# A mixture-of-experts layer and a Fourier layer: each row block's sum stays in on-chip memory from its gathers to its placing

## The chip, the cores and the metric

The kernel runs on one core of one Trainium2 chip. The metric is the device time in microseconds (us), the median of three runs. The engines are named as in the profile: PE multiplies matrices, PEld is its loading of weights, DVE, ACT and POOL work on vectors, and SP issues DMAs. On-chip memory has 128 partitions; DRAM is the memory outside. All arithmetic is float32.

## The reference

Two layers follow each other. The input `x` is 32 x 128 x 56 x 56.

```
layer 0:  x  = depthwise_conv7x7(input) + bias;  x = layernorm over channels -> xf [100352, 128]
          logits = xf @ Wg; the two best of 8 experts per token, softmax weights
          each expert takes at most cap = 15680 tokens, in order of priority -> slot of (token, choice)
          y  = gelu(buf @ W1[e] + b1[e]) @ W2[e] + b2[e]        per expert e, buf = rows of xf
          out0 = input + x + layer_scale * sum over 2 choices of  gate * y[slot]
layer 1:  feat = gelu(batchnorm(conv3x3, dilation 3 (out0)))     128 -> 64 channels
          F2   = fft2(feat); channel attention per head on F2; gate = sigmoid(two 1x1 convs of real(F2))
          out  = concat(|ifft2(attn @ F2)|, |ifft2(gate * F2)|) + out0
```

What this case is about is the line `out0`: for each token the normed row of `xf` and two rows of `y`, which lie at arbitrary slots, are added and transposed back to channels by pixels.

## The kernel before

**Layer 0.** The convolution, the norm and the routing leave `xf` (one row of 128 floats per token) and, after them, two lists `slot1` and `slot2`. The experts run one after the other in chunks of 512 slots: `first_layer` (L1071) and `second_layer` (L1089) on PE, GELU on ACT; `y`, already times its gate and the layer's scale, goes to the DRAM tensor `yf`. Row 0 of `yf` is zero, for tokens that found no room.

**Row blocks.** An image has 7 blocks of 8 rows; two images make a pair, 16 pairs in all, and block `r` (0 to 111) is the same 8 rows of both images of its pair: 7 tiles of 128 tokens. For each block `release` (L442) issues 14 gathers on POOL, one per call (L458: 128 rows of `yf` by `slot1` or `slot2`), into two tiles `y` of [128, 7, 128]. Ahead of a block's first gather it takes a tile `xa` from the pool `d6` and loads the block's rows of `xf` into it (L451, SP). `total` (L465) adds both `y` to `xa` on DVE (L474, two instructions of 896 elements in each partition) and stores the sum to the DRAM tensor `xsum` (L475, SP). Later `bring(r)` (L490) reads the block back from `xsum` into a tile `xs` of the pool `d3`, which has three buffers (L497, SP).

**Placing.** `place(r)` (L1282) transposes the 7 tiles of `xs` on PE (L1289) and adds them on DVE to the padded images `xp` (L1293), which then are the input of layer 1.

**Layer 1.** `front` places the 7 blocks of a pair and runs the 3x3 convolution on them (L1304). `back` is the Fourier part: `transform` alternates transposes on PE (L1347), copies from PSUM on DVE (`mid`, L1334), products on PE (L1355) and copies on ACT (L1358), four times; between them the attention (L1444, L1445) and the gate (L1482). The steps of the next pair's `front` are fed in between those of this pair's `back`. Outputs leave by SP (L1461, L1530).

**What sets the order.** PE, DVE, ACT and POOL each execute their own list in order, and so does SP for its DMAs. A planner places the instructions of a list by their dependencies; the kernel adds rules. `worked` (L482) counts columns of PE work and calls `release` once for each PACE of them (684 columns, L1543), then `totals`, which sums a block when the gathers asked for have passed its end by 7. Each gather waits on POOL for the PE instruction that was the newest when the gather 16 places earlier was asked for (`marks`, `gated`). In the last expert's chunks `ahead` (L505) releases gathers too, as far as the finished slots allow. If a block is to be brought and its gathers have not all been asked for, `total` asks for the missing ones at once (L468). The sums stand on DVE behind the newest DVE instruction named in `step["dve"]`.

Of the kernel before, what the change touches and what calls it, by code (L numbers as in the profile page):

```python
# [30 lines left out]
F32 = mybir.dt.float32  # L31
# [7 lines left out]
C = 128  # L39
# [6 lines left out]
E = 8  # L46
# [5 lines left out]
NB = H // P8  # L52
# [22 lines left out]
def conv_seq_kernel(ctx: ExitStack, tc: tile.TileContext, t: dict, out: bass.AP, dbg: dict):  # L75
    nc = tc.nc
    NI = t["xp"].shape[0]
    HI = NI // 2
    J = HI * NP
# [24 lines left out]

    xf = dram.tile([J * 128, C], F32, name="xf")
    yf = dram.tile([NSLOT + 1, C], F32, name="yf")
    xs_ = dram.tile([J * 128, C], F32, name="xsum")
    xl = dram.tile([-(-cap // 512) * 512, C], F32, name="xlast")
    xfv = xf.rearrange("(j p) c -> p j c", p=128)
    xsv = xs_.rearrange("(j p) c -> p j c", p=128)  # L110
    xlv = xl.rearrange("(j p) c -> p j c", p=128)


# [12 lines left out]
    with tc.tile_pool(name="a1", bufs=1) as a1, tc.tile_pool(name="a2", bufs=2) as a2, tc.tile_pool(  # L126
        name="a4", bufs=4
# [292 lines left out]
    begun_ = {}  # L420
    marks = []
    leash = {"n": 4}
    made_ = {"asked": 0, "summed": 0, "rows": 0}
    rows = {}
    step = {}
    work = {"since": 0}
# [15 lines left out]
    def release():  # L442

        n = made_["asked"]
        if n >= NRB * NG:
            return
        made_["asked"] += 1
        r, k = divmod(n, NG)
        if k == 0:
            xs = d6.tile([128, NB, C], F32, name="xa", tag="xa")  # L450
            nc.sync.dma_start(out=xs, in_=xfv[:, r * NB : (r + 1) * NB, :])  # L451
            begun_[r] = xs, []
        if k % NB == 0:
            begun_[r][1].append(d6.tile([128, NB, C], F32, name="y"))
        m = k % NB
        s = (slot1, slot2)[k // NB]
        marks.append(step["pe"])
        gated(marks[max(0, n - leash["n"])], nc.gpsimd.indirect_dma_start(  # L458
            out=begun_[r][1][-1][:, m, :],
            out_offset=None,  # L460
            in_=yf[: 1 + reach(r), :],
            in_offset=bass.IndirectOffsetOnAxis(ap=s[:, r * NB + m : r * NB + m + 1], axis=0),
        ))

    def total():  # L465

        r = made_["summed"]
        while made_["asked"] < (r + 1) * NG:  # L468
            release()
        made_["summed"] += 1  # L470
        xs, ys = begun_.pop(r)
        with tc.issue_after(step["dve"].ins):
            for y in ys:
                nc.vector.tensor_tensor(out=xs, in0=xs, in1=y, op=ALU.add)  # L474
        nc.sync.dma_start(out=xsv[:, r * NB : (r + 1) * NB, :], in_=xs)  # L475

    def totals(lag):

# [9 lines left out]
            totals(NB)  # L488

    def bring(r):  # L490
        if r >= NRB or r < made_["rows"]:
            return
        made_["rows"] = r + 1
        while made_["summed"] <= r:
            total()
        xs = rows[r] = d3.tile([128, NB, C], F32, name="xs")
        nc.sync.dma_start(out=xs, in_=xsv[:, r * NB : (r + 1) * NB, :])  # L497

    def inputs(pr):
        xps = [d4.tile([C, XL], F32, name="xp") for i in range(2)]  # L500
# [24 lines left out]
    if True:  # L525
# [649 lines left out]
        for e in range(E):  # L1175
            todo = late
            chain["on"] = e >= early
            if e + 1 < E:
                todo = todo + [due(1.4, lambda e=e: scale(e + 1))]
            if e in pairs:  # L1180
                todo = todo + search(*pairs[e])
            if e == E - 1:
                for s in late:
                    s()
                locate()
                lists_.close()
                rkey.__exit__(None, None, None)
                d4 = ctx.enter_context(tc.tile_pool(name="d4", bufs=4))
                d6 = ctx.enter_context(tc.tile_pool(name="d6", bufs=6))
                d3 = ctx.enter_context(tc.tile_pool(name="d3", bufs=3))  # L1190
                d0 = ctx.enter_context(tc.tile_pool(name="d0", bufs=1))
                first_inputs = inputs(0)
                bC = load(d0, "beta", [C, 1], t["ln_beta"].rearrange("(c o) -> c o", o=1))
                eps5 = d0.tile([128, 1], F32, name="eps5")
                norms = [[load(d0, n, [128, 5], t[n])] for n in ("bn1", "cgbn")]
                for i, n in enumerate(norms):
                    n += [d0.tile([128, 1], F32, name=f"{k}{i}") for k in ("scale", "shift")]
                cw = load(d0, "cw", [C, 9, DD], t["conv_w"])
                g1 = load(d0, "g1", [128, 32], t["cg1"])
                g2 = load(d0, "g2", [128, 128], t["cg2"])  # L1200
                g2b = load(d0, "g2b", [128, 1], t["cg2_b"])
                tau = load(d0, "tau", [128, 1], t["tau"])
                neg = load(d0, "neg", [128, 128], t["neg"])
                meanw = load(d0, "meanw", [128, 128], t["meanw"])
                rw = load(d0, "rw", [2 * W, 4 * KF], t["rw"])
                rh = load(d0, "rh", [2 * H, 4 * KF], t["rh"])
                ih = load(d0, "ih", [4 * KF, 2 * H], t["ih"])
                iw = load(d0, "iw", [4 * KF, 2 * W], t["iw"])
                todo = []
            if e + 1 < E - 1:  # L1210
                ids2, gates2 = lists()
                steps, late = listing(e + 1, ids2, gates2)
                todo = todo + steps
            elif e + 1 < E:
                (ids2, gates2), late = last, []
            if e == 0:
                todo = todo + search(E - 1, 1)
            if e == early - 1:
                last = [c1.tile([128, NC], d, name=n) for d, n in ((I32, "ids_last"), (F32, "gates_last"))]
                steps, done_ = listing(E - 1, *last)  # L1220
                todo = todo + steps + done_
            slots_ = len(chunks) * 4 - 18
            state = [0, 0, 0.0, 0]
            whole = sum(share.get(f, 0.7) for f in todo)

            def tick():
                state[0] += 1
                if e == E - 1:
                    state[2] += 1
                    ahead(i, state[2])  # L1230
                with tc.issue_after(step["dve"].ins):
                    while state[1] < len(todo) and state[2] * slots_ < state[0] * whole:
                        s = todo[state[1]]
                        if s in apart and state[3] == state[0]:
                            break
                        s()
                        state[2] += share.get(s, 0.7)
                        state[1] += 1
                        state[3] = state[0]

            for i, c0 in enumerate(chunks):
                if i + 1 < len(chunks):
                    then = fetch(ids, chunks[i + 1], e == E - 1)
                elif e + 1 < E:
                    then = fetch(ids2, 0, e + 1 == E - 1)
                if early <= e < E - 1 and i + (e - early) * len(chunks) < NC:
                    put(0, i + (e - early) * len(chunks))
                state[2] = 0 if e == E - 1 else state[2]
                if e == E - 1 and i == len(chunks) // 2:
                    batchnorms()  # L1250
                if e == E - 1 and i == len(chunks) - 1:
                    for r in range(2):
                        bring(r)
                ns, xT = now
                hT, gelu, mine = first_layer(e, ns, xT, tick)
                if left:
                    after, more = second_layer(*left, tick)
                    after(gelu)
                    mine = mine + more
                spots.append(mine + mine[-1:] * (8 - len(mine)))  # L1260
                left = e, c0, gates, ns, hT
                now = then
            assert state[1] == len(todo)
            if e + 1 < E:
                ids, gates = ids2, gates2
# [15 lines left out]

    def place(r, xps):  # L1282
        xs, rb = rows.pop(r), r % NB
        for m0 in range(0, NB, 4):
            nm = min(4, NB - m0)
            pt = bank("pxs")
            pv = pt[:, : nm * 128].rearrange("p (q m s) -> p q m s", m=nm, s=P8)
            for m in range(nm):
                nc.tensor.transpose(pv[:, :, m, :], xs[:, m0 + m, :], ident)  # L1289
            for i in range(2):  # L1290
                px = interior(xps[i], rb * P8, P8)[:, :, m0 * P8 : (m0 + nm) * P8]
                pi = pv[:, i * P8 : (i + 1) * P8].rearrange("p r m s -> p r (m s)")
                step["dve"] = nc.vector.scalar_tensor_tensor(  # L1293
                    out=px, in0=pi, scalar=bC, in1=px, op0=ALU.add, op1=ALU.add
                )
# [400 lines left out]
```

## Time and profile before

| | |
|---|---|
| median of three runs | 5173.07 us (5170.29 to 5176.02) |
| the profiled execution, its time / its span | 5216.56 us / 5214.8 us |
| mean granted PE clock | 0.943 of full speed |
| busy share of the span: PE, DVE, ACT, POOL | 89%, 54%, 40%, 50% |
| gathers of `y` on POOL (L458) | 1568, mean 990 ns |
| sums on DVE (L474) | 224 instructions, mean 1086 ns |
| `xa` loads, `xsum` stores, `xs` loads | 112 of each, 448 KB each |

One execution was profiled; its time is 43.5 us above the median of the runs that were timed without a profile. The last expert's gathers begin at 2605 us, the first placing stands at 2888 us, and the last gather starts at 5075.6 us. `back` runs L1403 once for each pair; from its first instance (2980.9 us) to its fifteenth (5042 us) lie 14 whole pairs. In rows of a stretch, the number behind an engine's busy time is its count of instructions in that stretch, "PEclk" is the mean granted clock, and "DMA" is the mean busy share of the 16 DMA engines.

### The profile page before, as it was taken

Reading aid. Unit: us, or ns where it says so; the run is one execution under the profiler, and the core shown is the slowest. Engines: PE = TensorE matmul, PEld = TensorE weight load, DVE = VectorE, ACT = ScalarE, POOL = GpSimd, SP = SyncE. Lnnn points to the kernel's source line nnn. Section 1 sums busy time; section 2 is a strip of 40 time slices with the busy share of each in tenths; the row PEclk is TensorE's granted clock in tenths of the full one; section 3 lists DMA queues with packets and bytes.
Section 4 is the critical chain, followed back from the end, with each engine's and each line's share of the span. In section 5 each row is a group of like instructions: output and inputs, shape, how many; then the busy total and the mean of one; then the engine's idle time right before and its main releaser. Section 6 shows DMA issues by size and latency. Waiting matters only on the chain.

```text
span 5214.8 us, 87254 instructions
## 1 busy us (share of the span) xinstructions
PE 4650.3 (89%) x33034; PEld 3232.1 (62%) x33034; DVE 2816.8 (54%) x5863; ACT 2079.1 (40%) x4260; POOL 2616.5 (50%) x2633
## 2 busy tenths in 40 slices
PE   8888845999999999999988899899988888888889
PEld 7777734777776777777766455555555555445556
DVE  4787887868675746442222345455544444444446
ACT  3676751444444444444433133333332222232224
POOL 0000023545555656666366566666666666665650
PEclk9999966999999999999999899999999999998999
DMA  9988840222222323333455456555555555555552
GB/s 255 271 260 262 262 127 26 65 64 66 68 69 71 86 76 85 88 86 93 149 156 133 115 158 163 155 149 149 147 154 152 155 155 158 150 130 146 157 142 57
DMA packets 767737, 705.23 MB, mean 135 GB/s; under 512 B 73232, under 2 KB 679569, under 8 KB 763221
## 3 DMA queue, kind: packets, MB, share of 16 engines
q1 hardware_dynamic: 597060, 487.55, 31.6%
q0 software_dynamic: 81664, 167.15, 14.6%
q10 hardware_dynamic: 88592, 44.96, 3.0%
q8 instruction: 261, 4.28, 0.4%
q14 instruction: 160, 1.30, 0.1%
HBM read 472.99 MB, written 226.39 MB: 134 GB/s over the span
## 4 chain that ended last, share of the span: by engine, by line
PE 70%; another core or an unknown queue 5%; issue 5%; DVE 4%; ACT 2%; DMA 0%; POOL 0%; DVEq 0%; ACTq 0%; POOLq 0%
PE py L1089 16%; PE ph L1071 15%; PE pf L1304 15%; PE pm L1355 9%; PE pt L1347 4%; PE pxt L1054 2%; PE pg L1379 2%; PE pre L1444 2%; PE pxs L1289 2%; PE pim L1445 2%; DVE junk L716 1%; PE pid L956 1%; PE pn L745 1%; DVE mid L1334 1%
## 5 line engine op out<-in xcount | busy, mean ns | idle before, releaser
L458 POOL DMA_INDIRECT y<-yf,slot x1568 | 1552.4, 990 | 971.3 <-issue 357.3
L1048 POOL DMA_INDIRECT xg<-xf,ids x861 | 906.9, 1053 | 689.2 <-PE py L1089 214.7
L1089 PEld LDWEIGHTS py<-W,hT 128*128 128x128 f32 x7872 | 928.9, 193 | 128.6 <-issue 108.2
L1089 PE MATMUL py<-W,hT 128*128 128x128 f32 x7872 | 948.7, 277 | 23.6 <-issue 23.3
L1304 PE MATMUL pf<-xp,cw 128*64 128x448 f32 x4032 | 926.7, 569 | 8.8 <-DVE xp L1293 6.1
L1071 PE MATMUL ph<-xT,W 128*128 128x512 f32 (+1 forms) x1984 | 907.3, 597 | 1.8 <-issue 1.8
L1074 ACT ACTIVATE hT<-ph,b1t 128x512 f32<-128x512 f32 (+1 forms) x992 | 616.2, 672 | 97.7 <-PE ph L1071 52.4
L1334 DVE COPY mid<-pt 112x512 f32<-112x512 f32 (+3 forms) x480 | 311.1, 662 | 570.5 <-PE pt L1347 239.4
L1123 ACT ACTIVATE yo<-yo,gates 128x128 f32<-128x128 f32 x861 | 275.3, 390 | 851.7 <-DVE yo L1103 782.3
L1103 DVE TENSOR_TENSOR yo<-py,b2t 128x512 f32<-128x512 f32 (+2 forms) x256 | 170.6, 669 | 790.1 <-issue 475.0
L1071 PEld LDWEIGHTS ph<-xT,W 128*128 128x128 f32 x1984 | 359.6, 193 | 339.2 <-issue 325.4
L1304 PEld LDWEIGHTS pf<-xp,cw 128*64 128x64 f32 x4032 | 289.8, 140 | 439.0 <-issue 394.7
L220 POOL TENSOR_SCALAR y<-y,sd,nb 128x128 f32<-128x128 f32 x49 | 24.8, 525 | 690.5 <-PE plq L277 689.2
L1358 ACT COPY T<-pm 128x464 f32<-128x464 f32 (+2 forms) x240 | 123.6, 520 | 494.3 <-PE pm L1355 282.6
L225 ACT ACTIVATE y<-y,nb,sd 128x128 f32<-128x128 f32 x735 | 287.6, 481 | 33.4 <-DVE nb L212 33.4
L1293 DVE SCALAR_TENSOR_TENSOR xp<-pxs,beta,xp 128x256 f32<-128x256 f32 x448 | 173.6, 445 | 169.7 <-remote 49.4
L174 PE MATMUL psa<-xt,stay 112*64 112x98 f32 (+1 forms) x4608 | 234.3, 262 | 34.6 <-DVE y L182 16.6
L174 PEld LDWEIGHTS psa<-xt,stay 112*64 112x64 f32 (+1 forms) x4608 | 220.0, 146 | 44.6 <-DVE y L182 23.1
L1312 ACT ACTIVATE feat<-pf,shift,scale 128x448 f32<-128x448 f32 x112 | 81.2, 725 | 411.7 <-remote 141.5
L474 DVE TENSOR_TENSOR xa<-xa,y 128x896 f32<-128x896 f32 x224 | 243.3, 1086 | 2.8
L1355 PE MATMUL pm<-ih,mid 116*128 116x112 f32 x928 | 151.0, 311 | 91.5 <-ACT T L1358 36.6
L1355 PEld LDWEIGHTS pm<-ih,mid 116*128 116x128 f32 x928 | 129.3, 215 | 165.9 <-issue 62.1
(410 smaller groups left out, 6241.9 us busy)
## 6 DMA issues: line engine op xcount, KB each, us to landing
xt<-in_x_dram SPq DMA_DIRECT2D x256, 392.0 KB
yf<-yo SPq DMA_DIRECT2D x240, 256.0 KB
xp<-in_xp_dram SPq DMA_DIRECT2D x32, 1832.0 KB
xa<-xf SPq DMA_DIRECT2D x112, 448.0 KB
xsum<-xa SPq DMA_DIRECT2D x112, 448.0 KB
xs<-xsum SPq DMA_DIRECT2D x112, 448.0 KB
xf<-y ACTq DMA_DIRECT2D x42, 1024.0 KB
y<-yf,slot POOLq DMA_INDIRECT x1568
```

The source lines that it names most:

```text
L174: nc.tensor.matmul(ps[h * 64 : (h + 1) * 64, c * TG : (c + 1) * TG], lhsT=wts[b][:, c4 + c, :], rhs=xv[: PKS[b], c, h, :, b * NB : b * NB ...
L225: nc.scalar.activation(yi, yi, AF.Identity, scale=sd[:, i : i + 1], bias=nb[:, i : i + 1])
L458: gated(marks[max(0, n - leash["n"])], nc.gpsimd.indirect_dma_start(out=begun_[r][1][-1][:, m, :], out_offset=None, in_=yf[: 1 + reach(r), :],
L474: nc.vector.tensor_tensor(out=xs, in0=xs, in1=y, op=ALU.add)
L1048: paced(2 * q, nc.gpsimd.indirect_dma_start(out=xg[:n, q, :], out_offset=None, in_=xf, in_offset=bass.IndirectOffsetOnAxis(ap=ids[:n, c0 + ...
L1071: step["pe"] = nc.tensor.matmul(ph[:, :ns], lhsT=W1[:, e, f * C : (f + 1) * C], rhs=xT[:, :ns], start=True, stop=True)
L1074: gelu = nc.scalar.activation(hT[:, f, :ns], ph[:, :ns], AF.Gelu, bias=b1t[:, e, f : f + 1])
L1089: step["pe"] = nc.tensor.matmul(py[:n, q * C : (q + 1) * C], lhsT=hT[:, f, q * 128 : q * 128 + n], rhs=W2[:, e, f, :], start=(f == 0), sto ...
L1123: nc.scalar.activation(yo[:n, q], yo[:n, q], AF.Copy, scale=gates[:n, c0 + q : c0 + q + 1])
L1304: step["pe"] = nc.tensor.matmul(pf[i * DD : (i + 1) * DD, : 8 * W], lhsT=cw[:, k, :], rhs=xps[i][:, o : o + 8 * RP].rearrange("p (h w) -> ...
L1334: step["dve"] = nc.vector.tensor_copy(to, of)
L1355: step["pe"] = nc.tensor.matmul(pm[:, i * M : (i + 1) * M], lhsT=mid[:m, i, :], rhs=by, start=True, stop=True)
```

## The change

The DRAM tensor `xsum`, its store and its load are gone. A block's sum stays in the tile `xa` from the first load to the placing. The tiles of `xa` move from `d6` (six buffers, which the tiles `y` keep) to a pool `d9` of nine, which takes the place of `d3` and of the six. A block's tile is free again when the block has been placed, so `release` now asks for no gather of a block that lies nine or more beyond the number placed. `bring(r)` only makes sure that the block's sum has been issued.

```diff
-    xs_ = dram.tile([J * 128, C], F32, name="xsum")
-    xsv = xs_.rearrange("(j p) c -> p j c", p=128)
...
-    made_ = {"asked": 0, "summed": 0, "rows": 0}
+    made_ = {"asked": 0, "summed": 0, "placed": 0}
+    HELD = 9
...
     def release():
         n = made_["asked"]
-        if n >= NRB * NG:
+        r, k = divmod(n, NG)
+        if n >= NRB * NG or r >= made_["placed"] + HELD:
             return
         made_["asked"] += 1
-        r, k = divmod(n, NG)
         if k == 0:
-            xs = d6.tile([128, NB, C], F32, name="xa", tag="xa")
+            xs = d9.tile([128, NB, C], F32, name="xa")
             nc.sync.dma_start(out=xs, in_=xfv[:, r * NB : (r + 1) * NB, :])
...
                 nc.vector.tensor_tensor(out=xs, in0=xs, in1=y, op=ALU.add)
-        nc.sync.dma_start(out=xsv[:, r * NB : (r + 1) * NB, :], in_=xs)
+        rows[r] = xs
...
     def bring(r):
-        if r >= NRB or r < made_["rows"]:
-            return
-        made_["rows"] = r + 1
-        while made_["summed"] <= r:
+        while made_["summed"] <= min(r, NRB - 1):
             total()
-        xs = rows[r] = d3.tile([128, NB, C], F32, name="xs")
-        nc.sync.dma_start(out=xs, in_=xsv[:, r * NB : (r + 1) * NB, :])
...
-                d3 = ctx.enter_context(tc.tile_pool(name="d3", bufs=3))
+                d9 = ctx.enter_context(tc.tile_pool(name="d9", bufs=HELD))
...
-                if e == E - 1 and i == len(chunks) - 1:
-                    for r in range(2):
-                        bring(r)
...
     def place(r, xps):
         xs, rb = rows.pop(r), r % NB
+        made_["placed"] = r + 1
```

## The prediction

> **What bounds the kernel now.** I read the page's slices first, then one row per stage, then the waits.
>
> ```profile
> span 5214.8 us, 87254 instructions
> ...
> PE   8888845999999999999988899899988888888889
> ...
> PEclk9999966999999999999999899999999999998999
> DMA  9988840222222323333455456555555555555552
> ```
>
> PE is busy nearly everywhere, so it is the bound; what matters is where it falls below 9 and where its clock does. That is from slice 20 (2600 us) on, where the gathers of `y`, the loads of `xa`, the stores to `xsum` and the loads back run. The row per stage, first in the experts' code, which is the same work in all four stretches:
>
> ```profile
> 2400.00:2500.00 100.00, 99.61 (x581) 73.27 (x580) 21.05 (x41) 49.83 (x109) 63.46 (x67) 1.00 0.35 94
> 2500.00:2600.00 100.00, 99.80 (x594) 73.86 (x593) 21.24 (x34) 50.29 (x111) 33.03 (x35) 1.00 0.49 146
> 2600.00:2700.00 100.00, 86.83 (x448) 60.61 (x447) 19.64 (x26) 37.79 (x80) 64.09 (x65) 0.91 0.62 172
> 2700.00:2800.00 100.00, 89.95 (x478) 64.10 (x476) 21.74 (x28) 37.67 (x80) 66.68 (x69) 0.93 0.57 144
> ```
>
> At a DMA share of 0.35 (with as many gathers on POOL as later) and of 0.49 PE gets through 581 and 594 instructions per 100 us at full clock; at 0.62 and 0.57 it gets through 448 and 478, a fifth fewer. Then layer 1, four pairs early, four late, and the last stretch, where the gathers have ended:
>
> ```profile
> 3118.80:3668.10 549.30, 504.16 (x2967) 303.47 (x2968) 277.74 (x478) 175.10 (x292) 346.11 (x343) 0.96 0.58 157
> 4268.80:4888.20 619.40, 532.75 (x2996) 319.38 (x2996) 285.73 (x487) 175.09 (x293) 384.29 (x393) 0.92 0.56 150
> 5042.00:5159.00 117.00, 114.59 (x716) 69.65 (x716) 60.13 (x107) 43.17 (x73) 23.33 (x24) 1.00 0.30 74
> ```
>
> PE's work per pair is the same (742 and 749 instructions), but a pair takes 137.3 us early and 154.9 us late. At the last stretch's rate (716 in 117 us) 746 take 122 us. So a pair holds 15 to 33 us in which PE is idle or at a lower clock. The waits of the late pairs say where:
>
> ```profile
> DVE mid L1334 <- remote: 63.0, 12, 12.5
> ...
> SPq L475 <- DVE xa L474: 159.2, 17, 21.9
> SPq L497 <- DMA xsum<-xa: 58.3, 24, 4.0
> ...
> PE pm L1355 <- DVE mid L1334: 27.2, 7, 8.4
> ```
>
> and one of those gaps, as the timeline has it for PE, DVE and SP:
>
> ```profile
> 4479.84 1.41 PE L1347 MATMUL pt<-ident,Z 128*116 128x128 f32 x11
> 4489.37 1.97 DVE L1334 COPY mid<-pt 116x512 f32<-116x512 f32 x3 [12.49 <-remote]
> 4490.11 2.05 PE L1355 MATMUL pm<-ih,mid 116*128 116x112 f32 x8 [8.40 <-DVE mid L1334]
> ...
> 4476.90 0.36 SPq L475 DMA_DIRECT2D xsum<-xa  x1
> 4480.00 0.36 SPq L497 DMA_DIRECT2D xs<-xsum  x1
> 4480.41 0.57 SPq L451 DMA_DIRECT2D xa<-xf  x1
> ```
>
> The transposes end by 4481.7, yet DVE sees them only at 4489.4; ACT resumes in the same 0.1 us. PE's signals come 8 us late, just after a store, a load back and an `xa` load in a row. Gathers are not what is waited for: the waits that stand before the sums (L474) last 50 ns at most, and the placing's transposes wait 12.7 us in all in layer 1 for nothing the profile names. I read this as PE being slowed by dense DMA traffic of short rows; the last three fences are consistent with it, none proves it.
>
> **The change, part by part.**
>
> *The 112 stores and 112 loads.* 200,704 packets of 512 B leave, of 767,737, and 100 MB of 705. The direct gain, PE's waits for the loads, is 0 to 12.7 us; I take 0. The indirect one is contention. One packet on SP's queue takes 0.316 x 16 x 5214.8 us / 597,060 = 44 ns of one DMA engine on average, so a block's 896 packets fill the 16 engines for 2.5 us, and a pair's 14 transfers for 34 us at most (the queue's mean includes longer packets; 31 ns, as in the stretch around 4480 us, gives 24 us). Now the DMA engines are busy 0.56 x 154.9 = 87 us of a late pair. Less 24 to 34 leaves 53 to 63, a share of about 0.43 of a pair of 134 us. The mean pair is 2061.1 / 14 = 147.2 us at a share of 0.57; the last stretch gives 122 us at 0.30. A straight line between them gives 134.1 us at 0.43. By the experts' rows (no loss at 0.49, though with half the gathers) it could be all of the way, 122; by the early and late pairs (nearly the same share, 17.6 us apart) it could be none, 147, or worse. I take the line: 14 x (147.2 - 134.1) = 183 us.
>
> The Trainium skill speaks against this ("DMA: Bandwidth & Descriptors", section "Rules for kernel authors"): issue a DMA early, compute, wait for it late, and its cost lies under the compute. The store and the load back are just such DMAs, sums stand 28 us or more ahead of their placing in the late pairs, and by that rule the part is worth 0 and the sum stays at 5173. The rows above weigh more with me: equal PE code a fifth slower where DMA is dense.
>
> *SP's queue.* With the store goes a wait on DVE's sums (159 us in four late pairs) behind which outputs (L1461, L1530) and `xp` loads stood. Who waits for these in turn is DVE, for a free output tile: the groups `oa` and `ob` show 25.4 and 29.4 us of idle time that nothing explains. DVE is busy half the time and not the bound: 0 to 10 us, I take 0.
>
> *The tile held to the placing.* An `xa` load now waits for PE's transposes of the block nine earlier instead of for a store. In the order of the changed program the first such load stands on SP right behind the second block's transposes, and later ones long after theirs: 0. The sum becomes ready where it was, 28 us or more before its placing, and no longer travels through DRAM: 0.
>
> *The smaller lead.* Counting calls of `release`: at the first placing 175 gathers have been asked for before, 126 after. A pair takes away 98, and the pace yields about 86, so the lead shrinks by 12 a pair, down to about 40, which `bring` keeps by asking for the missing gathers at once and summing right behind a placing. Before, this state begins near block 54 (about 3850 us, where pairs begin to take 150 us and more); after, near block 26 (about 3330 us). DVE's list of a pair is then the same as in the late pairs of before. If this state itself is the slow thing, the four pairs from 3391 to 3960 us, which take 142.3 us on average, go to 154.9: 4 x 12.6 = about +50 us. The early pairs, with lead, scatter their transfers; late ones have store, load and `xa` load in one burst after each sum. The change removes two of the three, so I take 0 and keep +50 as the rival below.
>
> *POOL.* 98 gathers at 990 ns and 0.30 us of issue between are 126.4 us a pair: a floor close below 134. Slack is one lag of 16 gathers, about 20 us. Cost 0 at 134; if DVE's in-order sums start to wait for gathers, everything behind them (`mid`, then PE) waits too.
>
> *The last expert.* There 49 gathers with three `xa` loads, three sums, 11 stores and 2 loads leave or come later. From 2600 to 2865 us PE loses about 20% (448 against 594), some 55 us, and 21.8 us at 2865 us. About a third of the packets of SP's queue goes; I take 17 us of these 77, bounds 0 and 60.
>
> Sum: 183 + 17 = 200 us. Profiled 5216.6 - 200 = 5017; the median lies 43.5 below its profiled execution, so **4973 us**.
>
> **The rivals.**
>
> *POOL takes over.* PE is relieved, but gathers at 126.4 us a pair plus their waits for PE's marks make sums late; pairs settle at about 141. For: POOL idles only 20% in layer 1 beyond its issue gaps. Against: its waits are mostly for PE, which would come sooner. 14 x 6 + 10 = 94 us gained: 5079. With smaller relief of any kind this is the case "faster by 10 to 100 us".
>
> *The lead was what kept pairs short* (slower than before). The early and late pairs have the same DMA share and the same PE work and differ in the lead alone that I can name. Then the slow state of 154.9 us begins at block 26 instead of 54: +50 us, 5223. It decides if removing two transfers of the burst gives back less than 50 / 11, some 5 us, per pair in that state. For: the sums stand right behind the placings there. Against: of some 21 us in which PE stands idle in a late pair, only about 3 have a sum on DVE in them or just ahead.
>
> *It is hidden anyway.* The lag of PE's signals has another cause that neither transfers nor lead touch: 5173, within 10 us.
>
> **How the numbers follow.** About 0.2% of this time, 10 us, is what its measurement can tell from no change. Chances: gain of 100 us or more, as forecast, 0.50; faster by 10 to 100 us 0.18; within 10 us 0.04; slower 0.28, most of it the lead. Faster 0.68, same 0.04, slower 0.28. The forecast's own range: pairs of 128 to 140 us with 0 to 60 in the last expert, 4850 to 5070. With the others, leaving out two in ten: 4890 to 5215.
>
> **What would show it.** The queue of SP has 200,704 packets fewer; DMA share near 0.43 in layer 1; DVE's waits for `mid` "remote" and PE's for `mid` shrink to a half or less; mean clock above 0.96; pairs (L1403 to L1403) of about 134 us with no step near 3850 us. The forecast is wrong if pairs take 150 us from about 3350 us on (the lead), if waits before the sums of several us appear (POOL), or if PE's late signals stay although the DMA share falls.

## The result, and the profile after

The changed kernel takes 5199.06 us in the median of 8 runs, the kernel before, run beside it, 5171.68 us: a ratio of 1.0050, 95% interval 1.0028 to 1.0072. The change makes the kernel slower by about 27 us. The forecast was 4973 us, 200 us faster.

The kernel before takes 5171 to 5173 us, as above, in three of the six groups of runs below, each timed on one chip (group A), and 4780 to 4784 us in the other three (group B; one chip was A once and B later), so only kernels of one kind are compared, each by its ratio to the kernel before in the same group.

Lines are those of each kernel: `mid` is copied at L1326 (L1334 before), the transposes `pt` stand at L1339 (L1347 before), the products `pm` at L1347 (L1355 before), the sums at L473 and the gathers at L457. A pair is counted from one instance of L1395 (L1403 before) to the next; I call these the pair marks, to tell them from the PE instructions, the marks of PE, that gathers wait for. The page of the changed kernel: clock and DMA share in 40 slices, and the queue of SP.

```profile
PEclk9999976999999999999999999999999998999999
DMA  9989840222222323333443344444343444434432
...
q1 hardware_dynamic: 392772, 384.77, 24.8%
```

SP's queue has 204,288 packets fewer; 200,704 of them are the stores and the loads back. The DMA share of layer 1 fell to 4 tenths. PE's rows did not follow. First the experts' code, then layer 1 (two early pairs, four after them, four late ones); the rows read as those of before.

```profile
2400.00:2500.00 100.00, 100.00 (x594) 74.41 (x594) 21.42 (x41) 50.73 (x108) 64.81 (x68) 1.00 0.35 96
2700.00:2800.00 100.00, 83.07 (x403) 56.72 (x402) 20.34 (x26) 33.47 (x72) 67.41 (x69) 0.90 0.38 94
2940.00:3219.00 279.00, 255.98 (x1514) 155.93 (x1511) 142.36 (x245) 87.03 (x146) 176.26 (x174) 0.95 0.44 117
3219.00:3808.00 589.00, 511.37 (x2989) 310.58 (x2988) 284.88 (x485) 174.87 (x292) 385.58 (x390) 0.94 0.43 113
4265.00:4875.00 610.00, 530.25 (x2980) 318.92 (x2980) 284.42 (x485) 173.92 (x292) 386.42 (x392) 0.92 0.41 110
```

The first two rows alone upset the forecast's reading: at nearly the same DMA share, 0.35 and 0.38, PE gets through 594 and 403 instructions. Share and PE's pace do not go together. POOL has as many instructions in both (68 and 69); in the first they are the gathers of the experts' input, in rows of four at most, in the second gathers of `y` have come in. In layer 1 a pair takes 139.4 us at first, 147.2 from the third pair on (3219 us), 152.5 late, at shares of 0.44, 0.43 and 0.41. The chain that ended last is still PE, at 70% of the span. The waits of the whole span:

```profile
DVE mid L1326 <- remote: 229.8, 42, 16.1
...
PE pm L1347 <- DVE mid L1326: 107.9, 37, 12.3
```

Both should have halved. They grew; before they were

```profile
DVE mid L1334 <- remote: 203.4, 45, 12.5
...
PE pm L1355 <- DVE mid L1334: 73.9, 29, 8.4
```

One of these waits in the changed kernel, in the order of time, with ACT, DVE, PE and POOL:

```profile
4015.87 1.52 PE L1339 MATMUL pt<-ident,Z 128*116 128x128 f32 x12
4024.17 0.95 POOL L457 DMA_INDIRECT y<-yf,slot  x1 [0.31 <-issue]
4026.16 0.72 ACT L1304 ACTIVATE feat<-pf,shift,scale 128x448 f32<-128x448 f32 x1 [17.34 <-remote]
4026.40 0.95 POOL L457 DMA_INDIRECT y<-yf,slot  x1 [1.28 <-remote]
4028.26 0.69 DVE L1326 COPY mid<-pt 116x512 f32<-116x512 f32 x1 [15.35 <-remote]
4029.01 2.05 PE L1347 MATMUL pm<-ih,mid 116*128 116x112 f32 x8 [11.62 <-issue]
```

and the stretch between as a row:

```profile
4017.40:4026.00 8.60, 0.00 (x0) 0.00 (x0) 0.00 (x0) 0.00 (x0) 5.88 (x7) 0.64 0.25 52
```

For 8.6 us nothing works on the core but POOL, which issues gathers, and the DMA queues hold nothing but these gathers (a share of 0.25). The transposes ended by 4017.4 by the record. ACT, POOL itself, which waits here for a mark of PE, and DVE get PE's signals 9 to 11 us later, the first of them about 1 us after POOL's row of gathers has stopped. There is no store, no load back and no `xa` load in it.

The gap that the prediction showed had such a burst just ahead of it; this one shows that no burst is needed. That gap, too, had a row of gathers in it, 22 of them from 4457.1 to 4486.6 us, which a timeline of PE, DVE and SP leaves out. Its last gather, and the first one after it:

```profile
4485.63 0.95 POOL L458 DMA_INDIRECT y<-yf,slot  x1 [0.30 <-issue]
4489.42 0.95 POOL L458 DMA_INDIRECT y<-yf,slot  x1 [2.84 <-remote]
```

POOL goes on in the same 0.1 us as DVE and ACT, 2.8 us after its row has stopped.

### The profile page after: what moved, and what is told of

Same layout as the page of the kernel before. It is cut to its first block, busy times and chain, and to the rows that moved or that the text cites. A ratio compares the mean times of both kernels' runs of the same rounds, so it can differ in the third digit from the quotient of the medians.

```text
span 5199.4 us, 86855 instructions
## 1 busy us (share of the span) xinstructions
PE 4635.2 (89%) x33034; PEld 3224.3 (62%) x33034; DVE 2812.2 (54%) x5863; ACT 2078.2 (40%) x4260; POOL 2620.8 (50%) x2633
## 4 chain that ended last, share of the span: by engine, by line
PE 70%; another core or an unknown queue 5%; issue 4%; DVE 3%; ACT 2%; POOL 1%; DMA 0%; DVEq 0%; POOLq 0%; ACTq 0%
PE py L1083 17%; PE ph L1065 16%; PE pf L1296 14%; PE pm L1347 9%; PE pt L1339 4%; PE pxt L1048 2%; PE pg L1371 2%; PE pre L1436 2%; PE pim L1437 1%; PE pxs L1281 1%; DVE junk L710 1%; POOL y L457 1%; PE pid L950 1%; PE pn L739 1%
## 5 line engine op out<-in xcount | busy, mean ns | idle before, releaser
L457 POOL DMA_INDIRECT y<-yf,slot x1568 | 1554.2, 991 | 962.8 <-issue 361.4
L1326 DVE COPY mid<-pt 112x512 f32<-112x512 f32 (+3 forms) x480 | 311.3, 662 | 630.6 <-PE pt L1339 315.2
L1347 PE MATMUL pm<-ih,mid 116*128 116x112 f32 x928 | 152.6, 312 | 121.7 <-DVE mid L1326 76.7
L1347 PEld LDWEIGHTS pm<-ih,mid 116*128 116x128 f32 x928 | 130.8, 216 | 194.6 <-DVE mid L1326 80.3
L473 DVE TENSOR_TENSOR xa<-xa,y 128x896 f32<-128x896 f32 x224 | 243.1, 1085 | 2.4
```

The costliest lines, as they stand in the source:

```text
L1326: step["dve"] = nc.vector.tensor_copy(to, of)
L1347: step["pe"] = nc.tensor.matmul(pm[:, i * M : (i + 1) * M], lhsT=mid[:m, i, :], rhs=by, start=True, stop=True)
```

## The experiments

### Is it the traffic or the lead?

The kernel before, with store and load back, and only the cap of the change:

```diff
-    made_ = {"asked": 0, "summed": 0, "rows": 0}
+    made_ = {"asked": 0, "summed": 0, "rows": 0, "placed": 0}
...
-        if n >= NRB * NG:
+        if n >= NRB * NG or n // NG >= made_["placed"] + 9:
...
-        xs, rb = rows.pop(r), r % NB
+        xs, rb, made_["placed"] = rows.pop(r), r % NB, r + 1
```

> The kernel before, with its store and load back kept, but with the cap of the change on the lead: no gather of a block is asked for that lies 9 or more blocks past the last one placed. Theory L (the lead: once the gathers asked for ahead have run out, the missing gathers of a block are asked for together, stand behind one mark of PE, run back to back on POOL, and PE's results come late): pairs of 146 us and more from about 3300 us on, as in the changed kernel, so 5200 to 5250 us. Theory T of the prediction (short-row DMA traffic slows PE; the lead costs nothing): traffic and pairs as before, 5172 us within 10. Theory P (gathers slow PE whatever their spacing): 5172 us within 10.

Group A: 5204.18 us, ratio to before 1.0058 (1.0039 to 1.0077). The changed kernel itself, timed again in another group A beside the kernel before:

> The changed kernel as it is, timed and profiled beside the kernel before once more, since two chips gave 5173 and 4784 us for the kernel before. Where that takes about 5173 us: 5199 us within 10, PE's results up to 15 us late. Where it takes about 4784 us (PE's results there come at once, gathers run back to back at 1.30 us each): theory G, a pair takes 120 us as long as it holds 86 to 91 gathers and 98 x 1.30 = 127 us where it must run all of its 98, and the change lets 49 fewer run before layer 1: +49 x 1.30 = 64 us of POOL in layer 1, less what the last expert no longer runs; 4790 to 4815 us. Theory T: the traffic taken away is worth something once PE is not held, below 4775 us.

5197.83 us, 1.0055 (1.0036 to 1.0073). So the smaller lead alone makes the loss, and the 200,704 packets, put back, change nothing that these intervals can tell (from the ratios, an estimate of 2 to 4 us, with some 15 us left open either way). The stretch of the late pairs with the packets back:

```profile
4264.00:4867.00 603.00, 521.45 (x2981) 312.57 (x2982) 284.00 (x484) 173.58 (x291) 389.39 (x393) 0.94 0.58 154
```

Four pairs in 603 us at a DMA share of 0.58; the changed kernel needs 610 at 0.41. Theory T, the forecast's own (dense DMA traffic slows PE), falls here.

### What holds PE's signals?

First no gathers in layer 1 at all. What is left out: the gathers issued once layer 1 has begun, in whose place the two sums add the tile to itself.

```diff
+        if leash["n"] == 16: return
         gated(marks[max(0, n - leash["n"])], nc.gpsimd.indirect_dma_start(
...
-                nc.vector.tensor_tensor(out=xs, in0=xs, in1=y, op=ALU.add)
+                nc.vector.tensor_tensor(out=xs, in0=xs, in1=y if leash["n"] == 4 else xs, op=ALU.add)
```

> The changed kernel without the gathers of layer 1: there the two sums of a block add the tile to itself, so its output is not the reference's from the blocks on whose gathers would have been issued in layer 1. L and P: PE's results come at once (lag near 0.06 us, as in the last stretch) and pairs take 117 to 124 us: 14 x (149 - 121) = 390 us less than the changed kernel, about 4800 us. If PE's late results have nothing to do with gathers (xa loads, outputs, PE itself): pairs of 140 us or more, 5080 us or more.

Group A: 4789.32 us, 0.9254 (0.9224 to 0.9284), and every pair from the third to the fourteenth 121.4 or 121.5 us. The gathers hold PE: 5199 - 4789 = 410 us in all. Then the same bytes into the same tiles, but as plain loads on SP's queue (other rows than the reference's are added), bound to the same marks:

```diff
+        if leash["n"] == 16:
+            return gated(marks[n - 16], nc.sync.dma_start(
+                out=begun_[r][1][-1][:, m, :], in_=yf[(n % 64) * 128 : (n % 64) * 128 + 128, :]))
```

> The changed kernel with each gather of layer 1 replaced by a plain load of 128 consecutive rows on SP's queue, as in the earlier run of that edit (4734 us where the kernel before takes 4780). Where the kernel before takes about 5172 us: if PE's results are late through POOL's gathers, 4730 to 4830 us, pairs of 118 to 125 us; if through the traffic into the tiles, whoever starts it, pairs of 140 us or more, 5080 us or more.

Group A: 4789.86 us, 0.9265 (0.9214 to 0.9315). Its row for three pairs:

```profile
4013.00:4377.00 364.00, 364.00 (x2235) 219.83 (x2234) 212.71 (x364) 132.40 (x219) 0.00 (x0) 1.00 0.48 138
```

PE is busy for all of the 364 us at full clock, at a DMA share of 0.48, more than the changed kernel's 0.41. It is not the bytes into the tiles; it is that POOL gathers them. (These loads read rows that follow one another, the gathers read scattered ones. Whether that or POOL's part in a gather matters was not tried.) The same edit in a group B, and one with a memset of the tile on POOL for each gather (which leaves the gathered rows out):

```diff
+        if leash["n"] == 16:
+            return gated(marks[n - 16], nc.gpsimd.memset(begun_[r][1][-1], 0.0))
```

> The changed kernel with each gather of layer 1 replaced by a plain load of 128 consecutive rows of yf on SP's queue, bound to the same mark of PE; its output is not the reference's. The bytes into the tiles stay, POOL has nothing to do in layer 1. Where PE's results come late: if they do so through POOL's gathers, pairs of 120 to 125 us, 4790 to 4830 us; if through the traffic into the tiles, whoever starts it, pairs of 140 us or more, 5080 us or more. Where they come at once: 4760 to 4810 us.

> The changed kernel with each gather of layer 1 replaced by a memset of the whole tile of gathered rows on POOL, bound to the same mark; its output is not the reference's. POOL is as busy with instructions, but starts no transfers. Where PE's results come late: if POOL's mere activity does it, pairs of 140 us or more, 5080 us or more; if it takes the starting of transfers, pairs of 120 to 125 us, 4790 to 4830 us. Where they come at once: 4760 to 4810 us.

They took 4733.89 us, 0.9898 (0.9878 to 0.9917), and 4728.61 us, 0.9887 (0.9867 to 0.9906), with pairs of 121.4 us both. As PE is not held in group B by gathers either (below), the memset doesn't tell whether POOL's activity without transfers would hold PE. That stays open.

### Asked for together, spaced, or too many?

Theory L said that a gather costs time when the lead has run out: the missing gathers of a block, asked for together, run in a row and so hold PE. Asking for more of them, so that none is ever missing:

```diff
-    PACE = (MAIN + FRONT) / (2 * NP) * 1.07
+    PACE = (MAIN + FRONT) / (2 * NP) * 0.95
```

> The changed kernel with gathers asked for 1.126 times as often in layer 1 (pace factor 0.95 for 1.07), so that 103 a pair are asked for where 98 are consumed, and the missing ones need not be asked for in blocks. Gathers, bytes and sums are the same. L: no step at 3219 or 3808 us, all pairs as the first two (139 us): 14 x (149 - 139) = 140 us less than the changed kernel, about 5060 us. T and P: the same traffic and the same gathers, 5199 us within 15.

Group A: 5237.47 us, 1.0128 (1.0098 to 1.0158): slower still. Counting the calls of `release` again, its lead stays between 56 and 82 gathers from the seventh block on (every sixth block was read), and no gather is missing when a block is summed. Yet its first two pairs take 145.4 and 146.0 us, where the changed kernel's take 139.3 and 139.5. What differs is how many gathers POOL runs in a pair. Counted between the pair marks of the profiles of group A, at a distance of 16:

| gathers run in a pair | pairs of | us a pair |
|---|---|---|
| 0 | no gathers; plain loads (from the third pair on) | 121.4 |
| 84 to 88 | before, changed, lead alone | 132 to 143 |
| 95 to 100 | before, changed, lead alone, faster asking | 145 to 156 |

From 86 or 88 gathers (first two pairs of the changed kernel, 139.4 us) to about 98 (the next twelve, 150.6 us on average) a pair grows by some 1 us for each. This is the step: the lead lets a pair run 86 gathers instead of 98, for as long as it lasts. How long the rows are (gathers with less than 0.6 us between them, counted in the traces) doesn't explain it at this distance: the late pairs of the kernel before have 10 to 28 of their gathers in rows of ten or more and take 153 to 156 us, those of the changed kernel from the third pair on have 29 to 46 and take 146 to 155 us.

Next the distance, how many gathers back the mark of PE lies that a gather waits for: 48 for 16.

```diff
-    leash["n"] = 16
+    leash["n"] = 48
```

> The changed kernel with each gather of layer 1 bound to the mark of PE 48 gathers earlier instead of 16: the same gathers, asked for at the same places, but POOL can run them back to back for three times as long. L (back-to-back gathers make PE late): pairs of 155 us or more throughout, 5230 to 5300 us. T and P: 5199 us within 15. If POOL's waits for PE were a cost themselves: faster than 5185 us.

Group A: 5789.34 us, 1.1190 (1.1157 to 1.1223), pairs of 178 to 200 us with as many gathers as ever. POOL now waits for a free tile (329.0 us for DVE's sums; 7.3 us in the changed kernel), then runs mostly 14, 21 or 28 gathers in a row. DVE's waits for `mid`, and one row of 21, with POOL, PE and DVE:

```profile
DVE mid L1326 <- remote: 629.6, 66, 23.9
```

```profile
4061.40 1.68 POOL L457 DMA_INDIRECT y<-yf,slot  x1 [15.50 <-DVE xa L473]
...
4061.34 1.05 PE L1347 MATMUL pm<-rw,mid 112*128 112x116 f32 x8
...
4072.20 1.24 PE L1339 MATMUL pt<-ident,T 128*112 128x128 f32 x9
...
4087.29 0.94 POOL L457 DMA_INDIRECT y<-yf,slot  x1 [0.30 <-issue]
4089.42 0.69 DVE L1326 COPY mid<-pt 112x512 f32<-112x512 f32 x1 [15.77 <-remote]
4090.17 2.05 PE L1347 MATMUL pm<-rh,mid 112*128 112x116 f32 x8 [15.83 <-DVE mid L1326]
4091.38 0.94 POOL L457 DMA_INDIRECT y<-yf,slot  x1 [3.15 <-DVE xa L473]
```

PE's transposes end by the record at 4073.4, 12 us into the row; DVE gets them at 4089.4, 1.2 us after the row's last gather. The price is paid twice: the eight products after the gap take 2.05 us at a granted clock of 0.50, the eight at the start of the row 1.05 us at 1.00. (That an idle window of about 3.4 us is enough for the half clock is stated in the Trainium skill, "TensorE: Matmul & The Clock Gate", section "Part 1: The HAM clock gate (the "warmup" mystery)"; PE's gap here is 15.8 us.)

Two more tiles for held sums, at the cost of two for gathered rows, to get part of the lead back:

```diff
-    HELD = 9
+    HELD = 11
...
-                d6 = ctx.enter_context(tc.tile_pool(name="d6", bufs=6))
+                d6 = ctx.enter_context(tc.tile_pool(name="d6", bufs=4))
```

> The changed kernel with two more tiles for held sums (11 for 9) and two fewer for gathered rows (4 for 6, two blocks' worth as the kernel before has), so that 154 gathers are asked for by the first placing (175 before, 126 in the changed kernel). Lead L or G (what was not gathered before layer 1 must be gathered in it): 28 / 49 of the loss comes back, 12 to 20 us faster than the changed kernel of the same chip, and the step to pairs of more gathers comes 2 pairs later. T, or a cost of the change that lies elsewhere (tiles held, order on SP's queue): no difference above 5 us.

Group A: 5501.69 us, 1.0640 (1.0622 to 1.0658). The longer lead came (224 gathers before the first pair mark for 196), and was buried: with four tiles POOL waits for a free one (282.7 us), and 784 gathers of layer 1 stand in rows of 14 or more, where the changed kernel has 285 and the run with a distance of 48 has 1298. No theory had foreseen it, since I had overlooked that these tiles also space the gathers. As a test of the lead it is spoilt. With the run before, it shows that on group A many rows of 14 and more cost hundreds of us, and that the table above does not hold for them: pairs of 84 gathers take 162 to 175 us here.

If the spacing alone decided (theory S; theory N is that the number of gathers does), 4 gathers of distance would bring most of it back:

```diff
-    leash["n"] = 16
+    leash["n"] = 4
```

> The changed kernel with each gather of layer 1 bound to the mark of PE 4 gathers earlier instead of 16, so that POOL can run fewer of them back to back; number, bytes and places of asking stay. Theory S (PE's results stall while POOL runs gathers back to back for more than some 6 us, so the spacing decides): shorter bursts, pairs of 128 to 142 us for 149, 5199 - 14 x (7 to 21) = 4900 to 5100 us. Theory N (only the number of gathers in a pair decides: 86 give 139 us, 98 give 150): 5199 us within 15. If the gathers become so late that sums wait for them: waits of several us before the sums and pairs of 150 us or more, 5220 us or more.

> The changed kernel with 4 gathers of distance for 16, once more, for a chip on which the kernel before takes about 5172 us. S (back-to-back gathers hold PE's results, the spacing decides; 48 gave pairs of 190 us and 16 pairs of 149): pairs of 128 to 142 us, 4900 to 5100 us. N (the number of gathers in a pair alone): 5198 us within 15. On a chip that takes about 4784 us: 4812 us within 6, as measured there.

> The changed kernel with 4 gathers of distance for 16. On a chip on which the kernel before takes about 5172 us: S, pairs of 128 to 142 us, 4900 to 5100 us; N, 5198 us within 15. On a chip that takes about 4784 us: 4815 us within 6, as twice before.

> The changed kernel with 4 gathers of distance for 16, a last time. On a chip on which the kernel before takes about 5172 us: S, pairs of 128 to 142 us, 4900 to 5100 us; N, 5198 us within 15. On a chip that takes about 4784 us: 4816 us within 6.

Three of these four fell on group B: 4812.26, 4817.21 and 4818.14 us, 1.0065 to 1.0067 with intervals inside 1.0048 to 1.0084. The last fell on group A: 5180.88 us, 1.0019 (1.0007 to 1.0032). That is some 17 us less than the changed kernel, not 100 to 300. S's forecast fails, and N misses its bound by 2 us. But the rows did not get shorter, so S was not put to the test below a distance of 16. Pairs, from the third on, stay at 145 to 155 us with 94 to 101 gathers, and POOL still runs rows of up to 27 (328 gathers in rows of 14 or more): at 98 gathers of 1.25 us from start to start it needs 122 us of a pair in which PE has work for 121, so that there is hardly room for pauses. Longer rows make it far worse; what shorter ones would do stays open.

### Group B

> The kernel before, profiled once more: its first profiled execution took 5216.6 us, 43 us above its median. If that execution was an outlier in layer 1, the pairs of this one are shorter (sum of the 15 pairs 2178 us there), the first mark of a pair again lies near 2981 us; if it was in the experts' part, the first mark lies near 2940 us and the pairs are as they were.

The kernel before once more, meant to explain its first profile, fell on group B: 4782.48 us, and says nothing on that. The changed kernel there:

> The changed kernel as it is, as reference for the others of this chip. Where the kernel before takes about 5172 us: 5198 us within 10. Where it takes about 4784 us: theory G (49 gathers more in layer 1 at 1.30 us of POOL each, which is the bound there) 4790 to 4815 us; theory T below 4775 us.

4799.14 us against 4780.38, 1.0037 (1.0025 to 1.0050). The same 500 us of layer 1, before and then changed, and what DVE waits for in the changed kernel's 500 us:

```profile
4100.00:4600.00 500.00, 481.11 (x2911) 288.83 (x2911) 277.87 (x474) 174.90 (x289) 383.01 (x384) 0.99 0.67 181
```

```profile
4100.00:4600.00 500.00, 483.46 (x2908) 287.91 (x2907) 279.70 (x479) 174.78 (x289) 382.57 (x386) 0.99 0.49 127
```

```profile
DVE xa L473 <- DMA y<-yf,slot: 59.5, 17, 6.8
DVE mid L1326 <- PE pt L1339: 50.1, 36, 5.7
```

No "remote" wait is left. Nor is PE by itself slower in group A: with plain loads for the gathers a pair takes 121.4 us in both kinds. In the changed kernel's layer 1, instructions of DVE and ACT that wait for PE alone start 0.05 us on average (0.42 at most) after the recorded end of what they wait for; in group A it was some 1.1 us (12.45 at most). Of the sums, 41 wait for gathers, 144 us in the whole span, of which there is nothing in group A. Here POOL is the bound of the late pairs: 98 gathers at 1.30 us make 127 us, and pairs of 97 to 99 gathers take 126 to 129. Pairs of up to 92 gathers take 120 to 124.

So the change loses here as well, and the account nearly closes. Up to the first pair mark 231 gathers run before, 196 after, and the mark comes 21.6 us sooner (2859.7 for 2881.3 us). Layer 1 has 35 more to run, and its 15 pairs take 1880.8 us for 1843.4, 37.4 more. The sum is 15.8 us; measured were 18.8.

Here the distance works the other way round. With 48:

> The changed kernel with 48 gathers of distance for 16. Where the kernel before takes about 5172 us: 5789 us within 25, as before. Where it takes about 4784 us: if long runs of gathers hold PE on every chip, 5100 us or more; if that is a property of the chips that take 5172 us, POOL only waits less for PE, 4780 to 4800 us.

4788.53 us, 1.0011 (1.0004 to 1.0018), on the chip that had been A earlier. With 1 (`leash["n"] = 1`), and the kernel before with 4 (`leash["n"] = 4`):

> The same with 1 gather for 16. S: bursts at their shortest, at or below the time of the run with 4 as long as sums do not wait; 4880 to 5100 us. N: 5199 us within 15. Late gathers: slower than the run with 4 by 10 us or more, with waits before the sums.

> The kernel before (store and load back, the longer lead) with 4 gathers for 16. S: the same gain as in the changed kernel, pairs of 125 to 140 us, 4900 to 5080 us; since the lead only shifts gathers out of layer 1, within 40 us of the changed kernel with 4. N: 5172 us within 15.

4852.92 us, 1.0152 (1.0128 to 1.0175), and 4798.44 us, 1.0031 (1.0018 to 1.0043). The tighter a gather is bound to PE, the more POOL, the bound, waits.

| distance, changed kernel | group A | group B |
|---|---|---|
| 1 | | 1.0152 |
| 4 | 1.0019 | 1.0065 to 1.0067 |
| 16 | 1.0050, 1.0055 | 1.0037 |
| 48 | 1.1190 | 1.0011 |

No version that computes what the reference computes beats the kernel before in either kind of group.

## Why the prediction was wrong

**"The 112 stores and 112 loads": 183 us, measured about nothing.** This is the step that failed. It took PE's late signals for an effect of the DMA share; what holds them is that POOL gathers, and the gathers stayed. The share came out as worked out (about 0.43), the packets are gone, and with the same lead the kernels with and without them take 5204 and 5198 to 5199 us. Leaving out the gathers of layer 1 gains 410 us. The straight line between two points of DMA share took the last stretch's quiet for an effect of its lower share. What had ended there were the gathers. The early and late pairs "nearly the same share, 17.6 us apart" said as much, and so did "though with half the gathers" beside the experts' row at 0.49; the one stood in the text as the lower bound, the other as a caveat, and neither was followed. The rule of the Trainium skill that spoke against the step ("DMA: Bandwidth & Descriptors", "Rules for kernel authors": issue early, wait late) gave 0 and was right here, for the whole of these transfers, where the page names the fixed setup cost.

**"The last expert": 17 us, measured 41, and by luck on the right side.** The first pair mark comes 41 us earlier in the profile (2940 for 2981). With the packets kept and only the cap added it comes at 2943. So some 38 of the 41 are the 51 gathers that no longer run before it (196 for 247), which layer 1 gets back, and not the packets. (Both figures rest on the one profile of the kernel before in group A, which ran long. In group B 35 gathers fewer brought the mark 21.6 us earlier.)

**"The smaller lead": taken as 0, measured 31 us.** This term was the second fault. The kernel before with the cap alone is 5204.2 - 5173.0 = 31 us slower. The rival "The lead was what kept pairs short" ended on the right side, with the place right (the step stands at the third pair, 3219 us, with block 26 placed in it) and the price too high (50 us). Its reason was wrong: neither the sums right behind the placings nor the asking at once is the slow thing, as the faster asking shows. Early and late pairs did differ in something besides the lead: the prediction's own rows have 343 instructions on POOL in four early pairs and 393 in four late ones. The lead is work done before layer 1. Each gather not done there costs about 1 us in layer 1 (in group A by the pairs of 86 and 98; 37.4 / 35 in group B), and saves less where it was.

**"SP's queue" and "the tile held": 0, right, but not as told.** The store's waits (463 us) went, and SP waits 851.2 us for PE's transposes at the `xa` load (L450) in their place, up to 34.8 us, where I had expected none. The outputs' waits for DVE (L1453) grew from 206.6 to 343.9 us. No sum waits for it (2.4 us of idle time before L473 in the whole span), and the kernel with the cap alone, which has no such waits at its `xa` loads, is no faster.

**"POOL": 0, right in group A.** No sum waits for a gather there. "POOL takes over" is what limits the late pairs in group B.

**"PE's late signals".** The observation was right and most of its reading wrong: it looked at the burst on SP and not at the row of 22 gathers in the same gap. The text's own test, that the signals stay late although the share falls, came true.

One thing can't be settled. The profiled execution of before (5216.6 us) lies above all 23 timed runs of it in the last group A (5149.5 to 5188.2). Its late pairs (154.9 us, against 152.5 of the changed kernel) are therefore no sign that the change relieved anything, and the 27 us can't be added up pair by pair in group A as in B.

## What to carry to other kernels

A correlation with the mean DMA share is not a cause: open one gap and list everything that still runs in it; here one engine and one queue were left. A lead on a stage is work done elsewhere at that place's price, so count the operations that a smaller lead pushes into the stage where they are dear, before costing the transfers that it saves. Time the kernel before beside every experiment: the setting that looked harmless in one kind of group (48, +0.1%) cost 12% in the other.

## What the runs showed of the hardware

- In three of six groups PE's results came late while POOL ran gathers in a row, and in none of the others, with the same programs. In the changed kernel's layer 1 DVE and ACT saw PE's results some 1.1 us late on average; PE saw DVE's, and DVE saw ACT's, after 0.03 to 0.06 us. In the run with distance 48, results that PE finished in the first 6 us of a row came less than 1 us late on average, those of 10 to 12 us into it 5 to 6 us, and many arrived only 1 to 3 us after the row's end.
- Loads of the same bytes from SP's queue never did it (PE busy 364.00 of 364.00 us), nor did the gathers of the experts' chunks from 900 to 1600 us, most of which stand alone (206 of 250 rows are a single gather): DVE and ACT saw PE's results after 0.04 us there.
- Group A shows in the trace itself. Wherever POOL gathers, a part of the semaphore updates is not on record: in layer 1 of the changed kernel 1598 of PE's 1854 are there, 1060 of DVE's 1718 and 637 of ACT's 1025. In group B, and on group A in layer 1 of the two runs that do not gather there, next to none is missing (at most 5 of 1025). It does not cost time by itself, since the experts' gathers show it too. But a wait that is called "remote" in group A can be one whose record is missing; the lateness above is taken from starts and ends of instructions and does not need it.
- Why a group is of one kind or the other, and what in a gather holds PE, the runs do not show. Whether PE itself stands still or only its signals do is open too. The memset on POOL, which would have narrowed it, was tried in a group B only.
